# Two graph-attention layers in one kernel: layer ends that add each half of a product from its own PSUM tile, an overflow table counted inside layer 1, and prelude weight steps placed one block later

## The chip, the cores and the metric

The kernel runs on one core of a Trainium2 chip. The metric is the device time of one execution in microseconds (us), and of several executions the median is taken. Inside a profile, times are counted from the first instruction of the execution.

## The reference

There are N = 2708 nodes with 1024 features each, and an adjacency matrix `adj` of 2708 x 2708 integers, about 17 neighbours to a node. Two attention layers follow each other, and each ends with a residual and a layer normalisation. Cut to what matters:

```python
f = x @ Wf + bf;  g = x @ Wg + bg            # layer 0
e = relu(f @ g.T)
attention = softmax(where(adj > 0, e, NEG), axis=1)
x = layernorm(x + attention @ (x @ W + bW))

h = x @ W1                                   # layer 1
e = leaky_relu(h @ a1 + (h @ a2).T, 0.2)
attention = softmax(where(adj > 0, e, NEG), axis=1)
x = layernorm(x + relu(attention @ h))
```

## The kernel before

The matrix is sparse, so nothing of size N x N is multiplied. The kernel turns each row of `adj` into a list of up to 40 neighbour numbers, sorts the nodes by the length of their lists, cuts them into 22 blocks (the first of 20 nodes, held in 32 rows, then 21 of 128), and gathers the neighbours' rows from memory. A block has four groups of 32 nodes. One gather brings 128 rows of 1024 numbers: 4 neighbours for each of the 32 nodes of a group. In total there are 405 such gathers in each layer.

Five engines work, each on its own queue in the order in which the program names the instructions (the class `InOrder` pins that order). In the profile nearly all instructions bear line 71, the line of that class, so they are told apart by their tiles.

- **Prelude** (the loop over `b` under `steps = weights()`). `lists(b)` loads a block of 128 rows of `adj` (three buffers), takes its relu and row sums on ScalarE, multiplies it with a ramp of column numbers on GpSimd (line 409), and takes the 40 largest values of each row on VectorE (`nc.vector.max` and `match_replace`, lines 412 to 418). `keep_lists` writes finished lists to memory from ScalarE. Beside it the generator `weights()` folds the weights: M = Wf Wg^T, and the vectors that come from the biases and from a1 and a2. It transposes on TensorE, copies out of PSUM on ScalarE, and multiplies on TensorE. It is cut into 21 steps by `yield`; the loop takes one step after each `lists(b)`, starting with block 0. The last steps are the rows for the bias (`c_product(1)`, cut in three by `row_parts` on GpSimd), eight transposed quarters of W1 (`turned`), and `u_product`.
- **Sort.** On the finished counts, VectorE and TensorE compute each node's place (line 452 to 499), which yields `ids`, the node numbers of each block.
- **Layer 0** (loop over `units`, order 1, 0, 2, ..., 21). `load_x` gathers the block's own rows, `x_turn` transposes them, `f_product` multiplies with M, `replicate` copies the result four times, `dots` takes one scalar product for each gathered tile on VectorE, and `soft` makes the softmax weights `st`. `sums` multiplies the same gathered tiles with `st` on TensorE into `po`; ScalarE scales that into `y`; `turn` transposes `y` (ScalarE copies it into `yTs`), and a `product` with W gives `Wp[b]`. `close(b)` adds the residual (`load_residual`), normalises (`norm`), takes the scalar products with `u1b` and `u2b` (`dot`, one instruction each on VectorE), writes the row to `X1S`, and scatters row and scalar product into the table `T1`. Each block's product and `close` run one unit late: `back` is the block before. The gathers go through a ring of 20 slots (`lay.gathers()`), and a slot is free when `sums` is done with it.
- **Layer 1** gathers from `T1`, whose rows carry their score, so `scores1` needs no scalar products. `sums`, `turn` and a `product` with M (which now holds W1) follow, then `close1`: relu, residual, `norm`, and a scatter into the output. The ring has 32 slots (`ring` and `more`). The first gather of layer 1 can't start before the last scatter into `T1` has landed.
- **Overflow test.** The lists have room for `TILES[g]` entries in each group. At the end of layer 1 the table `over` is set to 1 where a list must hold nothing (88 `memset`s on GpSimd), multiplied with the lists and counted on VectorE, summed on TensorE and copied by ScalarE into `flag`. All engines then read `flag` (`values_load`) and jump over the general path, which is only taken for other graphs.

A `product` makes both halves (512 columns each, one PSUM bank each) in one tile `pm` of the pool `ps_m`, which has two buffers. A reader of the tile waits for the whole tile. At the end of a layer the whole of the last product is therefore on the way before the residual is added:

```python
        Wp[b] = product(nrows[b], yTs.pop(b)[0], Wt, 32)
        ...
            dve.tensor_add(z[:n, :D], flat(Wp.pop(b))[:n], z[:n, :D])
            steps = norm(z, n)
```

Of the kernel before, what the change touches and what calls it, by code (L numbers as in the profile page):

```python
# [8 lines left out]
F32 = mybir.dt.float32  # L9
# [3 lines left out]
ALU = mybir.AluOpType  # L13
AX = mybir.AxisListType
# [43 lines left out]
TILES = [SORTED[_g] for _g in GROUPS]  # L58
# [48 lines left out]
def listed_path(ctx, tc, x, adj, Wf, bf, Wg, bg, W, bW, W1, a1, a2, out):  # L107
# [86 lines left out]
    with tc.tile_pool(name="pre", bufs=1) as pre:  # L194
# [54 lines left out]
        with tc.tile_pool(name="adjp", bufs=3) as adjp, tc.tile_pool(name="cands", bufs=2) as cands, \  # L249
# [185 lines left out]
            for b in range(NB):  # L435
                lists(b)
                if b > 2:
                    keep_lists(b - 3)
                if b == 4:
                    fill_highs()  # L440
                next(steps, None)
            for b in range(NB - 3, NB):
                keep_lists(b)
            for _ in steps:
# [96 lines left out]
    def half_product(pm, h, n, xT, w, row=None):  # L541
# [3 lines left out]
        for k in range(KC):  # L545
            pe.matmul(pm[:n, h, :], xT[:, k, :n], w[:, k, c],
                      start=(row is None and k == 0), stop=(k == KC - 1))

    def split_product(xT, w, parts, row=None):

        pm = ps_m.tile([P, H, 512], F32, name="pm")
        for h in range(H):
            c = slice(h * 512, (h + 1) * 512)
            if row is not None:
                pe.matmul(pm[:32, h, :], ones3[row:row + 3, :32], rows3[row:row + 3, c], start=True, stop=False)
            for k in range(KC // Q):
                for p in range(Q):
                    i = p * KC // Q + k  # L560
                    pe.matmul(pm[32 * p:32 * p + 32, h, :], xT[:, i, :32], w[:, i, c],
                              start=(k == 0 and (row is None or p > 0)), stop=(k + 1 == KC // Q))
        act.copy(parts, flat(pm))
        yield
        pm = ps_m.tile([P, H, 512], F32, name="pm")
        for h in range(H):
            pe.matmul(pm[:, h, :], rep, parts[:, h * 512:(h + 1) * 512], start=True, stop=True)
        return pm
# [13 lines left out]
            out=table, out_offset=bass.IndirectOffsetOnAxis(ap=idx, axis=0), in_=src,  # L582
            in_offset=None, bounds_check=N - 1, oob_is_err=False)

    def norm(z, n):


        st = small.tile([P, H, 6], F32, name="bst")
        mv = small.tile([P, 2], F32, name="mv")
        for h in range(H):  # L590
            dve.bn_stats(st[:n, h, :], z[:n, h * 512:(h + 1) * 512])
        dve.bn_aggr(mv[:n], st[:n])
        var, r, t = (small.tile([P, 1], F32, name=s) for s in ("var", "rstd", "newton"))
        dve.tensor_scalar(var[:n], mv[:n, 1:2], EPS, None, op0=ALU.add)
        ri, ti = r.bitcast(I32), t.bitcast(I32)
        dve.tensor_scalar(ti[:n], var.bitcast(I32)[:n], 1, None, op0=ALU.logical_shift_right)
        dve.tensor_scalar(ri[:n], ti[:n], -1.0, float(0x5F3759DF), op0=ALU.mult, op1=ALU.add)
        for _ in range(3):
            dve.tensor_scalar(t[:n], var[:n], r[:n], r[:n], op0=ALU.mult, op1=ALU.mult)
            dve.tensor_scalar(t[:n], t[:n], -0.5, 1.5, op0=ALU.mult, op1=ALU.add)  # L600
            dve.tensor_scalar(r[:n], r[:n], t[:n], None, op0=ALU.mult)
        sh = small.tile([P, 1], F32, name="sh")
        dve.tensor_scalar(sh[:n], mv[:n, 0:1], r[:n], -1.0, op0=ALU.mult, op1=ALU.mult)
        yield
        act.activation(z[:n, :D], z[:n, :D], AF.Identity, bias=sh[:n], scale=r[:n])
# [141 lines left out]
    with ExitStack() as s0s:  # L747
# [10 lines left out]
        def load_x(b):  # L758
            xb[b] = xp.tile([P, D], F32, name="xb") if b > 0 else zs[:, :D]
            gather(pool, xb[b][:nrows[b]], x, ids[:nrows[b], b:b + 1])  # L760

        def dot(a, v, n, col):
            j = jp.tile([P, D], BF16, name="j")
            dve.scalar_tensor_tensor(j[:n], a, 1.0, v[:n], op0=ALU.mult, op1=ALU.mult, accum_out=col)
# [52 lines left out]
        def close(b):  # L817

            n, m, z = nrows[b], valid[b], Z.pop(b)
            dve.tensor_add(z[:n, :D], flat(Wp.pop(b))[:n], z[:n, :D])  # L820
            steps = norm(z, n)
            next(steps)
            yield
            for _ in steps:
                pass
            sp.dma_start(X1S[start[b]:start[b] + m, :], z[:m, :D])
            yield
            dot(z[:n, :D], u1b, n, f1[:n, b:b + 1])
            dot(z[:n, :D], u2b, n, z[:n, D:D + 1])
            yield  # L830
            if z is not zs:
                pool.memset(z[:, D + 1:], 0.0)
            scatter(T1[:, :], ids[:m, b:b + 1], z[:m])
# [9 lines left out]
        load_lists(0)  # L843
        q_dot(1)
        q_dot(0)
        lay.most = len(units[0].tiles)
        first_gathers(1, 5)
        x_turn(1)
        spread0, spread1 = q_spread(0), q_spread(1)
        next(spread1)  # L850
        load_x(2)
        load_lists(2)
        lay.most += len(units[1].tiles)
        first_gathers(0, 1)
        x_turn(0)

        halves, xT = [], xTs.pop(1)
        for h in range(H):
            halves.append(ps_m.tile([P, H, 512], F32, name="pm"))
            half_product(halves[h], h, P, xT, M, 0)  # L860
        pool.memset(zs[:, D:], 0.0)
        load_lists(3)
        next(spread0)
# [27 lines left out]
        for k, u in enumerate(units):  # L891
# [18 lines left out]
            next(closing, None)  # L910
            for r in reps[1:3]:
                replicate(nxt.b, r)
            lay.sums(u, po, {12: [lambda s=closing: [None for _ in s]]}, y[b])
            closing = iter(())
            if ahead is not None and not first:
                x_turn(ahead)
            if k + 3 < NB and not first:
                loaded = seq[k + 3]
                load_x(loaded)
            if back is not None:  # L920
                load_residual(back)
                if back > 0:
                    Wp[back] = product(P, yTs.pop(back)[0], Wt, 32)
                else:
                    Wp[back] = whole(split_product(yTs.pop(back)[0], Wt, frp.tile([P, D], F32, name="Fr"), 32))
# [11 lines left out]
            steps = turn(y[b], nrows[b], yT, halves=True)  # L937
            next(steps)
            yTs[b] = yT, steps
            if k + 4 < NB and not first:  # L940
                load_lists(seq[k + 4])
            if nxt is not None:
# [9 lines left out]
        load_residual(b)  # L952
        for _ in yTs[b][1]:
            pass
        Wp[b] = product(nrows[b], yTs.pop(b)[0], Wt, 32)
        for _ in closing:
            pass
        for _ in close(b):
# [3 lines left out]
    with ExitStack() as s1s:  # L962
# [38 lines left out]
        def close1(b):  # L1001
            m, xt, z = valid[b], x1[b % 2], z1[b % 2]
            sp.dma_start(xt[:m], X1S[start[b]:start[b] + m, :])
            dve.scalar_tensor_tensor(z[:m], flat(prod.pop(b))[:m], 0.0, xt[:m], op0=ALU.max, op1=ALU.add)
            for _ in norm(z, m):
                pass
            yield
            scatter(out, ids[:m, b:b + 1], z[:m])

        lay.gathers()  # L1010
        scores1(units[0])
        closing = iter(())
        waiting = []
        for k, u in enumerate(units):
            nxt = units[k + 1] if k + 1 < len(units) else None
            b = u.b
            back = b - 1 if b > 0 else None
            po = ps_s.tile([P, H, 512], F32, name="po")
            y[b] = yp.tile([P, D], F32, name="y1")
            if back is not None:  # L1020
                for _ in yTs[back][1]:
                    pass
            lay.sums(u, po, {6: [lambda s=closing: [None for _ in s]]}, y[b])
            closing = iter(())
            if back is not None:
                if back > 0:
                    prod[back] = product(P, yTs.pop(back)[0], M)
                else:
                    prod[back] = whole(split_product(yTs.pop(back)[0], M, z1[1]))
            yT = tp.tile([P, KC, P], F32, name="yT")  # L1030
            steps = turn(y.pop(b), nrows[b], yT, halves=True)
            next(steps)
            yTs[b] = yT, steps
            if waiting:
                closing = close1(waiting.pop())
                next(closing)
            if back is not None:
                waiting.append(back)
            if nxt is not None:
                scores1(nxt)  # L1040
        for _ in closing:
            pass
        b = NB - 1
        for _ in yTs[b][1]:
            pass
        prod[b] = product(nrows[b], yTs.pop(b)[0], M)
        for b in waiting + [b]:
            for _ in close1(b):
                pass


        over = ovp.tile([P, NG, QT], F32, name="over")
        pool.memset(over, 0.0)
        for g in range(1, NG):
            if TILES[g] < QT:
                pool.memset(over[:, g, TILES[g]:], 1.0)
        for q in range(Q):
            pool.memset(over[32 * q:32 * q + valid[0], 0, TILES[0]:], 1.0)
        dve.scalar_tensor_tensor(over, SL, float(N), over, op0=ALU.is_lt, op1=ALU.mult)
        dve.tensor_reduce(bad[:, 0:1], over, AX.XY, ALU.add)  # L1060
        dve.tensor_reduce(bad[:, 0:1], bad, AX.X, ALU.add)
        pt = ps_t.tile([P, 4, P], F32, name="pt")
        pe.matmul(pt[0:1, 0, 0:1], bad[:, 0:1], ones, start=True, stop=True)
        act.copy(flag, pt[0:1, 0, 0:1])
    return nc.values_load(flag[0:1, 0:1])


@with_exitstack
def general_path(
# [360 lines left out]
```

## Time and profile before

| what | value |
|---|---|
| median of 3 runs | 1803.02 us (1797.66 to 1807.29) |
| span of the profiled execution | 1799.5 us |
| prelude | about 0 to 207 us |
| sort and first block | about 207 to 282 us |
| layer 0 | about 282 to 1173 us |
| layer 1 up to its last gather | about 1178 to 1726 us |
| what follows the last gather | about 1726 to 1799.5 us |
| busy: PE, DVE, ACT, POOL | 1573.3, 1172.8, 636.4, 1187.0 us |

The stages have different limits, and so the shares over the whole span (TensorE 87%) say little; each part of the change has to be read in its own stretch. In the rows of a timeline the columns are start, duration, engine, line, operation with output and input, count, and in brackets how long the engine had been idle and what ended that. A row of several instructions gives their time in sum or from first to last. "PEld" are the weight loads of TensorE. POOL is GpSimd; `DMA_INDIRECT` on POOL is the issue of one gather or scatter. In the chain of waits a row is start, duration, and the work or transfer that the end depended on.

### The profile page before, as it was taken

The numbers are of one execution on the slowest core, as the hardware profiler recorded it, in microseconds if no ns is written. First come the engines' busy times: TensorE is split into PE (matmuls) and PEld (weight loads), VectorE is DVE, ScalarE is ACT, GpSimd is POOL, SyncE is SP. The second block draws the span as 40 slices with busy tenths as digits, with TensorE's granted clock in tenths as the row PEclk, the third lists the DMA queues.
The fourth block names the chain that finished last, engine by engine and source line by source line (L and its number), as shares of the span: only waits on it lengthen the run. The fifth ranks groups of instructions, "written<-read, shape, count | busy, mean of one in ns | idle before, by whom it ended". The sixth has DMA issues, their size and how long they took to land. (4 is left out here: it accounts for less than half of the span.)

```text
span 1799.5 us, 22910 instructions
## 1 busy us (share of the span) xinstructions
PE 1573.3 (87%) x7313; PEld 669.9 (37%) x7313; DVE 1172.8 (65%) x3537; ACT 636.4 (35%) x861; POOL 1187.0 (66%) x1191
## 2 busy tenths in 40 slices
PE   5999279899999999999999997828989889889995
PEld 3544124343444443444444443303333333333332
DVE  4879737888888888888888887422442433433442
ACT  5545354444445545445554444101111111111110
POOL 7888476567666666766666653067777777777741
PEclk9999679899999999999999998959999999999997
DMA  7747068568777777777777786189999999999960
GB/s 267 262 151 261 20 238 303 209 211 292 292 262 263 261 262 260 278 276 287 289 293 275 260 292 227 71 339 368 362 394 393 393 360 396 392 391 381 370 229 26
DMA packets 149982, 501.86 MB, mean 279 GB/s; under 512 B 32565, under 2 KB 32597, under 8 KB 147144
## 3 DMA queue, kind: packets, MB, share of 16 engines
q0 software_dynamic: 132032, 427.36, 64.2%
q1 hardware_dynamic: 10202, 55.72, 8.2%
q10 hardware_dynamic: 7618, 17.23, 2.7%
q8 instruction: 59, 0.97, 0.2%
q14 instruction: 71, 0.58, 0.1%
HBM read 509.64 MB, written 33.75 MB: 302 GB/s over the span
## 5 line engine op out<-in xcount | busy, mean ns | idle before, releaser
L71 POOL DMA_INDIRECT ring<-in_x_dram,SL x405 | 439.9, 1086 | 258.2 <-issue 97.9
L71 DVE SCALAR_TENSOR_TENSOR j<-ring,Fr 128x1024 bf16<-128x1024 f32 x402 | 495.2, 1232 | 81.8 <-DMA ring<-in_x_dram,SL 55.6
L71 ACT COPY Fr<-pm 32x1024 f32<-32x1024 f32 (+2 forms) x353 | 340.7, 965 | 21.0 <-PE pm L71 16.3
L71 PE MATMUL po<-ring,st 128*32 128x512 f32 x2660 | 340.6, 619 | 0.1
L71 POOL DMA_INDIRECT ring<-T,SL x260 | 259.4, 998 | 84.9 <-issue 57.2
L71 PE MATMUL pm<-M,xT 128*128 128x512 f32 (+1 forms) x704 | 311.5, 622 | 0.4 <-ACT xT L71 0.4
L71 PE MATMUL pm<-Wt,xT 128*128 128x512 f32 (+1 forms) x704 | 303.5, 599 | 0.0
L71 PE MATMUL pm<-M,yT 128*128 128x512 f32 (+1 forms) x704 | 298.5, 595 | 0.3 <-ACT yT L71 0.3
L71 ACT ACTIVATE scores<-scores 128x24 f32<-128x24 f32 (+5 forms) x44 | 9.8, 222 | 667.7 <-DVE scores L71 667.7
L71 PEld LDWEIGHTS pm<-M,xT 128*128 128x128 f32 (+1 forms) x704 | 127.3, 191 | 172.1 <-issue 171.4
L71 PEld LDWEIGHTS pm<-M,yT 128*128 128x128 f32 (+1 forms) x704 | 127.2, 186 | 170.2 <-issue 169.7
L71 PEld LDWEIGHTS pm<-Wt,xT 128*128 128x128 f32 (+1 forms) x704 | 125.0, 186 | 151.8 <-issue 151.6
L71 POOL DMA_INDIRECT more<-T,SL x145 | 144.7, 998 | 44.6 <-issue 32.6
L71 PEld LDWEIGHTS po<-ring,st 128*32 128x32 f32 x2660 | 104.9, 115 | 185.6 <-issue 182.4
L71 DVE TENSOR_SCALAR scores<-ring,f1q 128x2 f32<-128x2 f32 (+5 forms) x98 | 21.7, 241 | 209.9 <-DMA ring<-T,SL 208.3
L409 POOL TENSOR_TENSOR adj<-adj,iota 128x2708 f32<-128x2708 f32 (+3 forms) x23 | 130.5, 5686 | 21.5 <-ACT adj L71 21.4
L71 ACT ACTIVATE y<-po,ri 128x512 f32<-128x512 f32 (+1 forms) x88 | 55.9, 684 | 221.4 <-PE po L71 203.9
L412 DVE MAX8 cand<-adj 128x8 f32<-128x136 f32 (+2 forms) x440 | 96.6, 285 | 36.3 <-POOL adj L409 36.3
L71 PE MATMUL pt<-rs,stack 128*32 128x1 f32 x680 | 13.8, 177 | 118.0 <-DVE rs L71 68.8
L71 PE MATMUL pm<-halfT,WfT 128*128 128x512 f32 x256 | 112.5, 594 | 1.5 <-ACT WfT L71 1.5
L71 POOL DMA_INDIRECT SL<-LD,idq x85 | 86.0, 1012 | 25.8 <-issue 20.9
L71 PE MATMUL po<-more,st 128*32 128x512 f32 x580 | 91.7, 639 | 0.0
(198 smaller groups left out, 1411.9 us busy)
## 6 DMA issues: line engine op xcount, KB each, us to landing
adj<-in_adj_dram SPq DMA_DIRECT2D x21, 1354.0 KB, 6.0
X1S<-z SPq DMA_DIRECT2D x20, 512.0 KB, 6.3
ring<-in_x_dram,SL POOLq DMA_INDIRECT x405, 6.4
u1b<-X1S SPq DMA_DIRECT2D x11, 512.0 KB, 7.1
rb<-X1S SPq DMA_DIRECT2D x10, 512.0 KB, 7.2
ring<-T,SL POOLq DMA_INDIRECT x260, 7.3
rows<-in_L_gnn_Wg_dram ACTq DMA_DIRECT2D x8, 512.0 KB, 6.4
rows<-in_L_gnn_Wf_dram ACTq DMA_DIRECT2D x8, 512.0 KB, 3.4
```

Of the source, the lines that this page charges most:

```text
L71: made = self.tc.keep_in_program_order(op(*args, **kwargs))
L409: nc.gpsimd.tensor_tensor(k[:n, cut], k[:n, cut], iota[:n, cut], op=ALU.mult)
L412: nc.vector.max(cand[:n, s, :], k[:n, s * SEG:min((s + 1) * SEG, N)])
```

## The change

It has five parts, called A to E below.

- **A**, prelude: the step of `weights()` after block 0 is left out, so each step stands behind the relu of the next block in ScalarE's queue, and the last step comes after the loop.
- **B**, start of layer 0: the first seven gathers of the first unit are issued, then the own rows of block 2 (`load_x(2)`), then the other eight.
- **C**, end of layer 0: the transposed `y` of block 20 is copied out at once; the product of block 20 and the rest of `close(19)` come ahead of the sums of block 21, where before they came after them; the last product is made in two PSUM tiles, and each half is added and taken into the statistics (`bn_stats`) by itself; in `close` the scalar product with `u2b`, which the scatter into `T1` needs, comes ahead of that with `u1b`.
- **D**, the table `over`: it is marked by GpSimd in small groups of `memset`s between the gathers of layer 1, counted before the sums of block 12, and `flag` is read by the engines in unit 20.
- **E**, end of layer 1: the last product in two tiles as in C, and nothing is left to do after the last scatter.

```diff
@@ prelude
-                next(steps, None)
+                if b > 0:
+                    next(steps, None)
@@
+    def two_products(n, xT, w, row=None):
+        halves = [ps_m.tile([P, H, 512], F32, name="pm") for h in range(H)]
+        for h in range(H):
+            half_product(halves[h], h, n, xT, w, row)
+        return halves
@@
-    def norm(z, n):
+    def norm(z, n, made=None):
...
         for h in range(H):
+            if made is not None:
+                made(h)
             dve.bn_stats(st[:n, h, :], z[:n, h * 512:(h + 1) * 512])
@@ close(b)
-            dve.tensor_add(z[:n, :D], flat(Wp.pop(b))[:n], z[:n, :D])
-            steps = norm(z, n)
+            pm = Wp.pop(b)
+            def add(h):
+                c = slice(h * 512, (h + 1) * 512)
+                dve.tensor_add(z[:n, c], pm[h][:n, h, :], z[:n, c])
+            if b + 1 < NB:
+                dve.tensor_add(z[:n, :D], flat(pm)[:n], z[:n, :D])
+            steps = norm(z, n, None if b + 1 < NB else add)
...
+            dot(z[:n, :D], u2b, n, z[:n, D:D + 1])
             dot(z[:n, :D], u1b, n, f1[:n, b:b + 1])
-            dot(z[:n, :D], u2b, n, z[:n, D:D + 1])
@@ start of layer 0
-        lay.most = len(units[0].tiles)
+        lay.most = len(units[0].tiles) // 2
         first_gathers(1, 5)
...
         load_x(2)
+        lay.most = len(units[0].tiles)
+        lay.gathers()
@@ unit loop of layer 0
+            if nxt is None:
+                for _ in closing:
+                    pass
+                load_residual(back)
+                Wp[back] = product(P, yTs.pop(back)[0], Wt, 32)
             lay.sums(u, po, {12: [lambda s=closing: [None for _ in s]]}, y[b])
...
-            if back is not None:
+            if back is not None and nxt is not None:
                 load_residual(back)
...
             yTs[b] = yT, steps
+            if k + 2 == NB:
+                for _ in steps:
+                    pass
@@ after it
-        Wp[b] = product(nrows[b], yTs.pop(b)[0], Wt, 32)
+        Wp[b] = two_products(P, yTs.pop(b)[0], Wt, 32)
@@ layer 1 (close1 has an add(h) of the same kind)
+        def mark_over(b):
+            for g in groups[b]:
+                if g == 0:
+                    for q in range(Q):
+                        pool.memset(over[32 * q:32 * q + valid[0], 0, TILES[0]:], 1.0)
+                elif TILES[g] < QT:
+                    pool.memset(over[:, g, TILES[g]:], 1.0)
...
         lay.gathers()
+        pool.memset(over, 0.0)
         scores1(units[0])
...
+            if k == NB // 2 + 1:
+                count_over()
             lay.sums(u, po, {6: [lambda s=closing: [None for _ in s]]}, y[b])
...
+            for i in (2 * k, 2 * k + 1):
+                if i < NB:
+                    mark_over(i)
+            if k + 2 == NB:
+                unfit = nc.values_load(flag[0:1, 0:1])
...
-        prod[b] = product(nrows[b], yTs.pop(b)[0], M)
+        prod[b] = two_products(P, yTs.pop(b)[0], M)
...
-        over = ovp.tile([P, NG, QT], F32, name="over")
...
-    return nc.values_load(flag[0:1, 0:1])
+    return unfit
```

More of the change, by code (lines that the diff above doesn't have):

```diff
@@ L855, in listed_path @@
         x_turn(0)
[L857 to L860, printed above, removed]
+        halves = two_products(P, xTs.pop(1), M, 0)
         pool.memset(zs[:, D:], 0.0)
@@ L1003, in close1, with add @@
             sp.dma_start(xt[:m], X1S[start[b]:start[b] + m, :])
-            dve.scalar_tensor_tensor(z[:m], flat(prod.pop(b))[:m], 0.0, xt[:m], op0=ALU.max, op1=ALU.add)
-            for _ in norm(z, m):
+            pm = prod.pop(b)
+            def add(h):
+                c = slice(h * 512, (h + 1) * 512)
+                dve.scalar_tensor_tensor(z[:m, c], pm[h][:m, h, :], 0.0, xt[:m, c], op0=ALU.max, op1=ALU.add)
+            if b + 1 < NB:
+                dve.scalar_tensor_tensor(z[:m], flat(pm)[:m], 0.0, xt[:m], op0=ALU.max, op1=ALU.add)
+            for _ in norm(z, m, None if b + 1 < NB else add):
                 pass
@@ L1008, in close1, with count_over @@
             scatter(out, ids[:m, b:b + 1], z[:m])
+        over = ovp.tile([P, NG, QT], F32, name="over")
+        def mark_over(b):
[5 more added lines that the diff above has]
+                    pool.memset(over[:, g, TILES[g]:], 1.0)
+        def count_over():
+            dve.scalar_tensor_tensor(over, SL, float(N), over, op0=ALU.is_lt, op1=ALU.mult)
+            dve.tensor_reduce(bad[:, 0:1], over, AX.XY, ALU.add)
+            dve.tensor_reduce(bad[:, 0:1], bad, AX.X, ALU.add)
+            pt = ps_t.tile([P, 4, P], F32, name="pt")
+            pe.matmul(pt[0:1, 0, 0:1], bad[:, 0:1], ones, start=True, stop=True)
+            act.copy(flag, pt[0:1, 0, 0:1])
         lay.gathers()
+        pool.memset(over, 0.0)
         scores1(units[0])
@@ L1049, in listed_path @@
                 pass
-        over = ovp.tile([P, NG, QT], F32, name="over")
[L1053 to L1064, printed above, removed]
-    return nc.values_load(flag[0:1, 0:1])
+    return unfit
 @with_exitstack
```

## The prediction

> **What bounds the kernel now.** I read the 40 slices, then windows by stage, then the chain of waits, and the timeline where the chain changes engine.
>
> ```profile
> PE   5999279899999999999999997828989889889995
> POOL 7888476567666666766666653067777777777741
> ```
>
> TensorE (PE) is full in layer 0 (slices 6 to 24), nearly idle at the change of layers (slice 25), and GpSimd (POOL) stands at one constant level all through layer 1. The windows of layer 1 (window, length, busy time of PE, PEld, DVE, ACT, POOL with counts, clock, DMA share, GB/s) sharpen that:
>
> ```profile
> 1300.00:1420.00 120.00, 107.65 (x561) 43.72 (x560) 42.57 (x177) 15.94 (x30) 91.63 (x93) 0.94 1.01 393
> 1420.00:1540.00 120.00, 107.06 (x618) 44.88 (x620) 49.20 (x205) 15.79 (x32) 91.56 (x93) 0.99 0.99 382
> ```
>
> Each holds 93 POOL instructions, 120 / 93 = 1.29 us for each: 0.99 busy and the 0.30 that the timeline shows ahead of nearly each gather. So layer 1 is paced by the issue of gathers, and the DMA engines are about full too. What delays the first gather, or takes POOL's time between gathers, goes into the end. How a short memset lies between gathers is seen once, in layer 0:
>
> ```profile
> 259.37 1.02 POOL L71 DMA_INDIRECT ring<-in_x_dram,SL  x1 [0.30 <-issue]
> 260.39 0.12 POOL L71 MEMSET z<- 128x4 f32 x1
> 260.69 1.01 POOL L71 DMA_INDIRECT SL<-LD,idq  x1 [0.19 <-issue]
> ```
>
> The next issue begins 1.32 us after the last one, so this memset lay within the 0.30 and cost about 0.01. The chain at the change of layers (start, duration, what):
>
> ```profile
> 1122.64 9.72 PE po L71 x60
> 1132.36 14.76 PE pm L71 x34
> 1147.12 0.87 PE pt L71 x8
> 1147.99 14.78 PE pm L71 x34
> 1162.79 1.24 DVE ring L71
> 1164.05 1.30 DVE bst L71 x2
> ...
> 1169.99 1.25 DVE j L71 x2
> 1171.26 1.24 DVE j L71 x2
> 1173.37 3.44 DMA T<-ring,ids
> ```
>
> Sums of block 21, product of block 20, transposes, product of 21, addition, statistics, two scalar products, last scatter. The first product belongs to a block that was ready at 1111, while PE waited 11.1 us for the softmax of block 21 (the wait of the transposes' tile for DVE rs). The chain's end:
>
> ```profile
> 1778.00 1.24 DVE z L71
> 1779.26 1.30 DVE bst L71 x2
> ...
> 1785.39 0.97 POOL out_dram L71
> 1786.36 0.83 POOL over L71
> 1787.24 2.88 POOL over L71 x84
> 1790.57 1.06 DVE over L71
> ```
>
> After the last scatter (issued by 1786.36) come 7.0 us for the table, up to the flag at 1793.40, then the jump, to 1799.5. In the prelude, ScalarE's (ACT's) relus of the last two blocks:
>
> ```profile
> 181.55 2.47 ACT L71 ACTIVATE adj<-adj 128x2708 f32<-128x2708 int32 x1
> 188.33 2.46 ACT L71 ACTIVATE adj<-adj 20x2708 f32<-20x2708 int32 x1
> ```
>
> Both had their data already; they stood behind copies of the weight steps. The sort's first matmul ran at 207.09, after PE had waited 18.8 us for the counts. So lists, not weights, end the prelude, yet PE is busy 59.1 of 60 us from 60 to 120 and 57.3 from 120 to 180.
>
> **What the Trainium skill says.** "TensorE: Matmul & The Clock Gate", section on the HAM clock gate: an idle array falls to half its clock, and about 3.4 us of work release it. The trace agrees: after the 11.1 us of waiting the sums took 9.90 us for 60 matmuls (clock 0.70), where block 20's took 7.05 for 64 (clock 1.00). "DMA: Bandwidth & Descriptors", section on one DMA of the GpSimd path: the fixed cost is mostly the completion of the write, about 2 us. Here the scatter into T1, 1.00 us of issue, kept the next gather waiting 3.24 us more. "Runtime: NRT & Kernel Launch", section on instruction fetch: a jump out of the fetched window stalls until its target is fetched. Here PE's jump at 1794.0 took 4.35 us, the other engines' under 0.1.
>
> **The change part by part.**
>
> *C, order.* Block 20's transposes end at 1111.1. ACT is idle then (its last copies end at 1107.5), so two copies of some 0.6 us let the product begin at about 1111.5; its PSUM buffer is the one those copies had emptied. It takes 14.76, to about 1126.4, 4.1 us past the softmax (1122.3), since `sums` stands behind it. Then 0.3 + 7.05 for the sums at full clock (the product has kept PE busy): 1133.8. Now `y`, its transposes and copies lie bare, where before the other product covered them: in the first unit of layer 0 sums ended at 289.1 and the second half's transposed copy at 291.8, of which the product, starting with the first half, needs about 2.6. Then 14.7: 1151.1, against 1162.79: 11.7 saved. If the sums stay at 9.90 it is 8.9.
>
> Does DVE keep up? `close(19)` still adds at 1122; its scatter (1132.45, with the new order of dots 1.27 earlier) frees `z`, the residual of 20 lands by about 1140, `close(20)` runs 9.5 us (1147.16 to 1156.73 before), to about 1149.5. It is ahead of the second half at 1151.1, with little to spare.
>
> *C, halves.* After the last matmul DVE does half of 1.24 and one bn_stats of 0.65 in place of 1.24 + 1.30: 1.25 saved; the first half lies beside the second product. *C, dots.* One dot, 1.27, leaves the path of the scatter; `u1b` runs while the scatter is on its way. C together: 11.7 + 1.25 + 1.27 = 14.2 (8 to 15). As layer 1 is a steady issue from its first gather, all of it arrives.
>
> *E.* Halves again 1.25. The table's 7.0 us leave the end. POOL then reads the flag after its scatter (0.50 in the trace), jumps, and the end waits for the scatter's landing: issue begin + 4.2 as for T1, which is near the 1799.5 - 1793.4 = 6.1 us that still follow. PE's slow jump moves behind the norm. E together 8.3 (6 to 9).
>
> *D.* 88 memsets, 4.18 us, go between gathers, in one of 850 columns (0.83) and 11 groups of eight. Beyond the first they came every (4.18 - 0.83) / 87 = 0.039 us, so a group is 0.31, about the gap that hid the memset above. Net: 0.83 - 0.30, and little for the groups; I take 1.0. Lower bound 0, upper 4.2. Reading 1.0 rests on one memset in one gap. The count adds 2.25 us on DVE (1.05 + 1.04 + 0.16) ahead of block 12's sums; queued behind it are the reciprocal and `close1`, and PE waits for it with one small matmul. Who waits for PE is the gather that needs its slot: in units 2 to 4 a slot's next gather came 6 to 8 us after the sums began, so 2.3 us are hidden. The read of the flag stands on PE ahead of block 21's sums: 0.5 us, of which 0.3 was idle; on the other engines it lies in waits of over 2 us. I count 0.2.
>
> *A.* Gain: at the end, block 21's relu no longer stands behind block 20's relu (2.8 with its accumulator and list) and the `u_product` copies (3.5 and gaps): 188.33 - 181.6 = 6.7. Cost: at the start ACT waits for the second block's load before it issues the weights' loads, so PE, which began at 14.57, begins about 4.5 later (loads of 1354 KB pass in 5 us), and PE has few idle microseconds to recover it in. Also GpSimd's `row_parts` (6.7 us) now sit between the last two line-409 multiplications, which holds the gain under 5.6. I take 3.5 (from 6 gained to 2 lost). The `u_product` copies that now come last end before ACT is needed by the sort.
>
> *B.* DVE's dots begin 6 to 7 us earlier (they waited for block 2's rows, 9.3 us until 255.33). But PE's `f_product(2)` ends at 281.5, after the softmax at 280.2, and does not depend on them. Nothing gained: PE's work hides it.
>
> Sum: -14.2 - 8.3 + 1.2 - 3.5 = -24.8; 1803.0 - 24.8 = 1778.
>
> **The rivals.**
>
> 1. *The prelude gives nothing.* PE is the bound there and the 4.5 us at its start stay. For it: 59 of 60 us busy; against: PE waited 18.8 at the end. 1803 - 14.2 - 8.3 + 1.2 + 1 = 1783.
> 2. *GpSimd takes the table in full and the layer end saves less:* memsets drain the issue (4.2), PE stays cold (C at 9). For it: the issue paces layer 1; against: the memset at 260.39. 1803 - 9 - 8.3 + 4.4 - 3.5 = 1787.
> 3. *DMA paces layer 1* (share 1.01), so the memsets are free, and the prelude's lists gain 5.6: 1803 - 15 - 9 + 0.2 - 5.6 = 1774. Against it: the issue comes like a clock at 1.29 to 1.30, and the gathers land in 7.2 to 7.3 us at the median, hardly more than the 6.4 of layer 0.
> 4. *Slower:* each of twelve memset stretches costs a whole issue slot, 12 x 1.3 = 15.6, the prelude loses 4.5, the order of C gains nothing beyond halves and dots (2.5) as `close(20)` waits for its residual, E gains 6: 1803 + 15.6 + 4.5 - 2.5 - 6 = 1815. Against it: all of the above lines.
>
> **How the numbers follow.** Forecast 0.55, rival 1 0.15, rival 2 0.13, rival 3 0.14, rival 4 0.03. The predicted time is the forecast's, 1778. The range reaches from 1769 (rival 3 and 5 us for the spread of runs, which was 1797.66 to 1807.29) to 1790 (rival 2 and some of that spread). The limit of 0.5% is 1794; rivals 1 to 3 all lie below it, so faster 0.93, same 0.04, slower 0.03.
>
> **What would show each step right or wrong.** C: the product of block 20 in the gap before block 21's sums, those at about 7 us, and the last scatter into T1 near 1156 on a prelude that is 3.5 us earlier (1173.4 - 14.2 - 3.5). D: 93 issues in 120 us still, and gaps of 0.3 to 0.4 around the groups; gaps of 0.6 or more would be rival 2. A: the sort's first matmul near 203.5; near 208, rival 1. B: the first sums still right after `f_product(2)`. E: nothing but the jump after the last scatter, about 6 us. The forecast fails if the sums of block 21 stay at 10 us, or a wait for the residual appears ahead of the last addition.

## The result and the profile after

| | before | changed |
|---|---|---|
| median | 1802.55 us (6 runs, 1797.66 to 1812.86) | 1779.38 us (6 runs, 1775.26 to 1786.32) |
| ratio, 95% interval | | 0.9881 [0.9857, 0.9906] |
| span of the profiled execution | 1799.5 us | 1777.1 us |

The changed kernel is faster by 23.2 us, within 2 us of the forecast. The parts do not agree as well as the sum, as the same views show. First the page's 40 slices of the changed kernel, PE and POOL:

```profile
PE   4999479899999999999999999637989988989996
POOL 7878476467666666666666663177777777777740
```

The hole at the change of layers is still there (slices 26 to 28 of 40; before, it was deepest in slice 27, which the prediction calls 25), and layer 1 still stands at one level. Its windows (window, length, busy time with counts of PE, PEld, DVE, ACT, POOL, clock, DMA share, GB/s):

```profile
1300.00:1420.00 120.00, 111.90 (x640) 43.93 (x637) 46.98 (x193) 14.80 (x29) 92.72 (x133) 0.93 1.01 392
1420.00:1540.00 120.00, 108.63 (x571) 44.35 (x570) 44.24 (x179) 17.03 (x32) 92.26 (x108) 0.96 0.99 380
```

POOL's count is 133 and 108 where it was 93: the memsets. Its busy time has grown by 1.1 and 0.7 us, more than nothing. The timeline of POOL around two groups:

```profile
1202.19 0.99 POOL L71 DMA_INDIRECT ring<-T,SL  x1 [0.31 <-issue]
1203.19 0.80 POOL L71 MEMSET over<- 20x7 f32 x8
1204.58 1.00 POOL L71 DMA_INDIRECT ring<-T,SL  x1 [0.59 <-issue]
...
1248.96 0.99 POOL L71 DMA_INDIRECT ring<-T,SL  x1 [0.30 <-DVE rstd L71]
1249.95 0.37 POOL L71 MEMSET over<- 128x3 f32 x8
1250.47 1.00 POOL L71 DMA_INDIRECT ring<-T,SL  x1 [0.15 <-issue]
```

From gather to gather it is 1250.47 - 1248.96 = 1.51 us in place of 1.30, and 2.39 at the first group. Half of the gap before a gather remains behind a memset, so a group isn't hidden in it. At the end of layer 0, PE's timeline shows the order that C wanted:

```profile
1110.65 7.13 PE L71 MATMUL pm<-Wt,xT 128*128 128x512 f32 x16
1117.72 0.31 PE L71 MATMUL pt<-rs,stack 128*32 128x1 f32 x16
1117.87 7.05 PE L71 MATMUL po<-ring,st 128*32 128x512 f32 x60
1125.77 1.23 PE L71 MATMUL pt<-ident,y 128*128 128x128 f32 x8 [0.86 <-ACT y L71]
...
1134.63 7.13 PE L71 MATMUL pm<-Wt,xT 128*128 128x512 f32 x16
```

The product of block 20 fills the former gap, the sums of block 21 take 7.05 us (9.90 before), and only 0.86 us of waiting is left in the row. The chain of waits there (start, duration, what):

```profile
1127.34 4.29 DMA z<-in_x_dram,ids
...
1131.72 1.24 DVE z L71
...
1141.37 0.61 DVE ring L71
1142.01 0.69 DVE bst L71
1142.70 0.60 DVE ring L71
1143.33 0.70 DVE bst L71
...
1148.68 1.24 DVE j L71 x2
...
1150.70 5.88 DMA T<-ring,ids
```

It now runs through the residual of block 20 and `close(20)`. The timeline of DVE and POOL shows the wait for that residual, and the scatter of block 19 that stands ahead of its gather:

```profile
1131.72 1.23 DVE L71 TENSOR_TENSOR z<-pm,z 128x1024 f32<-128x1024 f32 x1 [8.30 <-DMA z<-in_x_dram,ids]
```

```profile
1122.35 1.87 POOL L71 DMA_INDIRECT T<-z,ids  x1 [18.03 <-DVE j L71]
1127.34 1.03 POOL L71 DMA_INDIRECT z<-in_x_dram,ids  x1 [3.13 <-DMA T<-z,ids]
```

`close(20)` frees DVE at 1141.37, when PE is nearly done (about 1141.8). The addition and statistics of the first half still stand in front of the second half, whose addition begins at 1142.70: 0.9 us after its product was ready. The last row of the chain is the surprise: 5.88 us for the scatter's transfer, where 3.44 stood before. At the end of the program:

```profile
1762.02 0.70 DVE z L71
...
1762.75 0.71 DVE bst L71
...
1768.61 0.70 POOL out_dram L71
```

Half a row is added in 0.70 us in place of 1.24, and the last scatter is the chain's last row. ScalarE's relus of the last two blocks of the prelude:

```profile
176.80 2.46 ACT L71 ACTIVATE adj<-adj 128x2708 f32<-128x2708 int32 x1 [3.96 <-DMA adj<-in_adj_dram]
189.30 2.46 ACT L71 ACTIVATE adj<-adj 20x2708 f32<-20x2708 int32 x1
```

Block 20's comes 4.75 us earlier than before and now waits for its data alone, block 21's 0.97 later, and the sort's first matmul, 207.09 before, is at 207.46. By stages, with three later executions that are told of below (us; each row is the time from the event of the row above it, and each column adds up to its span):

| up to | before | changed | `after_again` | `best` | `a_lead` |
|---|---|---|---|---|---|
| sort's first matmul, from the start | 207.09 | 207.46 | 205.65 | 203.83 | 204.03 |
| first sums of layer 0 | 74.47 | 72.67 | 72.85 | 72.55 | 72.35 |
| sums of block 20 | 806.71 | 800.06 | 807.64 | 807.70 | 808.95 |
| first gather of layer 1 | 89.34 | 77.19 | 77.68 | 75.48 | 77.24 |
| issue of the last scatter | 607.78 | 610.95 | 609.08 | 607.89 | 608.80 |
| end | 14.13 | 8.72 | 8.41 | 8.09 | 8.10 |

So four questions stood open: where 6.65 us inside layer 0 came from, which the change hardly touches; what A gives; why the scatter lands later; what D costs.

### The profile page after: what moved, and what is told of

Same layout as the page of the kernel before. It is cut to its first block, busy times and chain, and to the rows that moved or that the text cites. A ratio compares the mean times of both kernels' runs of the same rounds, so it can differ in the third digit from the quotient of the medians.

```text
span 1777.1 us, 22911 instructions
## 1 busy us (share of the span) xinstructions
PE 1573.1 (89%) x7313; PEld 667.6 (38%) x7313; DVE 1171.4 (66%) x3539; ACT 636.4 (36%) x861; POOL 1182.5 (67%) x1191
## 5 line engine op out<-in xcount | busy, mean ns | idle before, releaser
L71 POOL DMA_INDIRECT ring<-in_x_dram,SL x405 | 432.0, 1067 | 256.2 <-issue 89.0
L71 PE MATMUL pt<-rs,stack 128*32 128x1 f32 x680 | 14.1, 179 | 98.0 <-DVE rs L71 53.4
```

What stands on the lines that cost most here:

```text
L71: made = self.tc.keep_in_program_order(op(*args, **kwargs))
```

## The experiments

**Parts alone.** Three kernels were the kernel before with only A, B or C of the diff, the fourth with D and E; the fifth was the kernel before again.

> Only A: the weight step of the prelude stands behind the next block's relu, all else as before. Theory from the two traces: nothing, 1802 us within 2. The weight rows are then asked for 3 us later, TensorE makes its first product some 6 us later, and the lists' first stages lose what the earlier relus gain: the sort's first matmul stays within 1 us of 207.1. Rival, the prediction's own step: 3.5 us less, 1799, with that matmul near 203.5. Second rival: A carries part of the 8 us by which the changed kernel leads at the end of layer 0, so 1797 or less.

> Only B: seven gathers of the first tiles, the load of block 2's rows, then the other gathers. Theory: the first sums come 0 to 1.5 us earlier (281.6 before) and the time is 1801 to 1803 us. Rival: B sets another phase between gathers and sums and is what made layer 0 drift ahead by 6.7 us more before its last block; then 1794 to 1796, with the sums of block 20 starting near 1080 and not near 1088.

> Only C: the end of layer 0 (product of block 20 ahead of the sums of block 21, halves in two PSUM tiles, dot with u2b first). Theory: the last scatter of T1 is issued some 14.5 us earlier counted from the sums of block 20, some 2 us of it is given back in the wait for its landing, and the time is 1790 us (1788 to 1792), with block 20's sums where they were before (1088, within 2). Rival: C is also where the drift inside layer 0 comes from, then block 20's sums start near 1081 and the time is near 1783. Second rival: the wait gives back all but 8 us, 1795.

> Only D and E: overflow table in layer 1, halves at its end, layer 0 and prelude as before. Theory from the two traces: the memset groups between the gathers cost layer 1 3.7 us, the end gives 6.5 us, together 2.8 us less, 1800 us (1798 to 1801). Rival, the prediction's steps: groups 1.0 and end 8.3, 1795. Second rival: gathers are hidden behind TensorE in layer 1 and D is free while E is 6.5: 1796.

> The kernel before once more, for a second trace of it. If the 6.7 us by which the changed kernel gains inside layer 0 (from the sums of unit 5 to those of block 20) are a difference between executions, this trace has block 20's sums some us away from 1088.3, within 1081 to 1095, with no edit at all. If they belong to A, B or C, it repeats 1088 within 1 us. On a chip whose clock is throttled as in the four runs of single parts, the first sums come near 290 instead of 281.6, and layer 1 takes some 750 us instead of 610.

They went to a chip that grants TensorE a mean clock of 0.90 to 0.91 where the first one granted 0.95. The kernel before takes 2006.74 us there (median of all 75 runs; 1985.00 in the one run of `before_again`), and no part could be told from nothing in the time: A 0.9967 [0.9928, 1.0006], B 1.0021 [0.9984, 1.0059], C 0.9963 [0.9915, 1.0012], D with E 1.0026 [0.9988, 1.0065]. PE's timeline in layer 1 of the run with A shows why C and D couldn't count there:

```profile
1601.60 11.00 PE L71 MATMUL pm<-M,yT 128*128 128x512 f32 x25
1613.55 0.59 PE L71 MATMUL pm<-M,yT 128*128 128x512 f32 x1 [0.95 <-issue]
...
1617.08 0.59 PE L71 MATMUL pm<-M,yT 128*128 128x512 f32 x1 [1.54 <-issue]
1619.18 1.01 PE L71 MATMUL pm<-M,yT 128*128 128x512 f32 x1 [1.51 <-issue]
```

Single matmuls of the product stand 1 to 1.5 us apart with nothing that they wait for. TensorE paces layer 1 on that chip: in the 120 us from 1240 GpSimd waited 16.4 us for TensorE's sums (15.2 to 20.6 us in the other four traces of that chip, 1.8 in the kernel before on the first chip), and there were 75 POOL instructions where 93 had been. An earlier first gather is then only waiting. `before_again` met the same chip, with block 20's sums at 1131.5, so its own question stayed open there. Distances inside a trace are what these runs can tell:

- C: from the sums of block 20 to the first gather of layer 1 77.34 us, against 89.05, 89.47, 88.20 and 87.70 in the four kernels without it. From the issue of the last scatter to that gather 6.67, against 4.2 to 4.4 in the others. So both the gain and what is given back come with C.
- E: from the last scatter to the end 8.36 us, against 13.98 to 14.41.
- Layer 0 from its first sums to those of block 20: 839.1 (the kernel before), 852.0 (D with E, which leave layer 0 as it was), 845.4 (B), 849.5 (C), 863.3 (A). One and the same code differs by 13 us here. The rival that A, B or C carries the 6.65 us had no support: none of the three had a shorter stretch than the kernel before.

**The scatter's landing.** Three edits of the changed kernel. `u1_first` undoes one part of C:

```diff
-            dot(z[:n, :D], u2b, n, z[:n, D:D + 1])
             dot(z[:n, :D], u1b, n, f1[:n, b:b + 1])
+            dot(z[:n, :D], u2b, n, z[:n, D:D + 1])
```

> The changed kernel with one part of C undone: the dot with u1b again ahead of the dot with u2b. Measured from the issue of the last scatter into T1 to the first gather of layer 1, which was 4.24 us before and 6.68 after the change. Theory: what follows the scatter so closely (the dot with u1b on DVE, and the 512 KB load into u1b that this dot releases) slows its descriptors or its data; here both are out of the way ahead of it, so 4.2 us again, the scatter 1.27 us later, and the first gather some 1.2 us earlier than in the changed kernel: about 76.0 us after the start of block 20's sums instead of 77.2. Rival: the longer wait comes with C's order (the write of X1S or the chain's place), then 6.7 stays and the first gather is 1.2 us later, 78.4.

`u1_late` holds the last block's dot with `u1b` behind the scatter:

```diff
             dot(z[:n, :D], u2b, n, z[:n, D:D + 1])
-            dot(z[:n, :D], u1b, n, f1[:n, b:b + 1])
+            if b + 1 < NB:
+                dot(z[:n, :D], u1b, n, f1[:n, b:b + 1])
...
             scatter(T1[:, :], ids[:m, b:b + 1], z[:m])
+            if b + 1 == NB:
+                pool.memset(f1[:n, b:b + 1], 0.0)
+                dot(z[:n, :D], u1b, n, f1[:n, b:b + 1])
```

> The changed kernel with the last block's dot with u1b held until GpSimd has issued the last scatter into T1 (a memset of its result column stands behind the scatter on GpSimd). Theory: the scatter has neither the dot nor the load beside it, so its issue is 1.0 and not 1.34 us and the whole 4.2 to 4.6 us instead of 6.68; first gather about 75 us after the start of block 20's sums instead of 77.2. Rival: the wait belongs to the write of X1S, still 2 us ahead, then 6.7 stays.

`x1_late` moves only the load:

```diff
-            sp.dma_start(xt[:m], X1S[start[b]:start[b] + m, :])
+            (act if b == 1 else sp).dma_start(xt[:m], X1S[start[b]:start[b] + m, :])
```

> The changed kernel with the load of block 1's rows of X1S into u1b asked for by ScalarE where the block is closed, instead of by SyncE as soon as the dot with u1b is done; the dots stay as they are. Theory of the load: its 512 KB share the DMA engines with the scatter's 522 KB, so the time from scatter issue to first gather falls from 6.68 to 4.3 to 4.6. Theory of the dot: [...]6.7 stays with the issue at 1.34. If both share in it, about 5.5.

The timeline of the changed kernel first, all engines, then POOL in `u1_late` and in `x1_late`:

```profile
1149.94 1.23 DVE L71 SCALAR_TENSOR_TENSOR j<-ring,u1b 128x1024 bf16<-128x1024 f32 x1
1150.70 1.34 POOL L71 DMA_INDIRECT T<-ring,ids  x1 [8.33 <-DVE j L71]
...
1151.20 0.33 SPq L71 DMA_DIRECT2D u1b<-X1S  x1
...
1157.38 1.03 POOL L71 DMA_INDIRECT ring<-T,SL  x1 [5.34 <-DMA T<-ring,ids]
```

```profile
1232.54 1.00 POOL L71 DMA_INDIRECT T<-ring,ids  x1 [8.32 <-DVE j L71]
1233.54 0.11 POOL L71 MEMSET f<- 128x1 f32 x1
1236.85 1.03 POOL L71 DMA_INDIRECT ring<-T,SL  x1 [3.20 <-PE pt L71]
```

```profile
1236.36 1.34 POOL L71 DMA_INDIRECT T<-ring,ids  x1 [8.32 <-DVE j L71]
1240.93 1.03 POOL L71 DMA_INDIRECT ring<-T,SL  x1 [3.23 <-DMA T<-ring,ids]
```

| | scatter's issue | then waiting | issue to first gather | block 20's sums to first gather |
|---|---|---|---|---|
| before | 1.00 | 3.24 | 4.24 | 89.34 |
| changed | 1.34 | 5.34 | 6.68 | 77.19 |
| `u1_first` | 1.00 | 3.49 | 4.49 | 77.02 |
| `u1_late` | 1.00 | 3.20 | 4.31 | 75.25 |
| `x1_late` | 1.34 | 3.23 | 4.57 | 75.18 |

The load is the cause of 2.1 us: with the dot where it was and only the load gone, the wait is 3.23 again. SyncE asks for 512 KB into `u1b` as soon as the dot has read it, half a microsecond after the scatter's issue began, and the two transfers share the engines. The Trainium skill ("DMA: Bandwidth & Descriptors", section "Issuing engines are not separate DMA queues") says just this: DMAs started by different engines run on the same DMA engines and interleave. The dot itself costs the 0.34 us of longer issue, which is absent wherever it doesn't run beside the scatter. That agrees with one rule of the Trainium skill's "SBUF — State Buffer", section "Who interferes with whom": a VectorE instruction with two SBUF inputs contends with a GpSimd instruction that reads SBUF. The dot is such an instruction. But the same section infers that a `tensor_tensor` with two such inputs leaves the writing of DMA descriptors alone; here the measurement decides, and what in the issue was held is not shown. The longer the two run together, the longer the issue: 0.47 us beside the dot gave 1.34, and in the changed kernel the scatters of blocks 19 and 20, 0.98 and 0.99 us beside their dots, took 1.87 and 1.86 (1.02 before). So the new order of the dots has a second price, which the prediction left out: from the issue of block 19's scatter to the gather of block 20's residual it was 4.99 us in place of 3.67, and DVE waited for that residual. `u1_first` came 0.17 earlier where 1.2 was expected, as its scatter was issued 2.02 us later and not 1.27: the old order also holds block 19's scatter, and with it the residual of block 20 and `close(20)`, so that the last dots began 0.66 later already. The new order of the dots is thus worth 2.0 us at the scatter; in the changed kernel all of it goes to the load's collision, in `x1_late` 1.8 remain (77.02 - 75.18).

**The table.** `table_early` is the changed kernel with all 88 memsets ahead of `lay.gathers()` and no `mark_over`:

> The changed kernel with all memsets of the overflow table ahead of layer 1's gathers, so that they fall in GpSimd's wait for the landing of the last scatter (5.34 us, against 4.18 us of memsets), and none between gathers. Theory: the 3.7 us that D cost in layer 1 are gone: gathers 1.30 us apart from the first on, the first gather still 6.7 us behind the scatter. Rival: the table's place is still held by layer 0, or the memsets hold up the landing, and the first gather comes up to 4.2 us later, which gives the gain back.

```profile
1269.15 1.34 POOL L71 DMA_INDIRECT T<-ring,ids  x1 [8.33 <-DVE j L71]
1270.49 4.17 POOL L71 MEMSET over<- 128x850 f32 x88
1275.60 1.04 POOL L71 DMA_INDIRECT ring<-T,SL  x1 [0.95 <-DMA T<-ring,ids]
```

The memsets lie whole within the wait: 6.45 us from scatter to gather (6.68 without them), 77.32 from block 20's sums, and the next 20 gathers 1.30 us apart. The rival falls. These four runs were on a third chip, with clocks of 0.897 to 0.913 and 1992 to 2046 us beside 2069 for the kernel before, one run each, so nothing is read from their times.

**All together.** `best` is the changed kernel with the edit of `x1_late` and the memsets on DVE, between `f1q` and the first gathers:

```diff
+        over = ovp.tile([P, NG, QT], F32, name="over")
+        dve.memset(over, 0.0)
+        for g in range(1, NG):
+            if TILES[g] < QT:
+                dve.memset(over[:, g, TILES[g]:], 1.0)
+        for q in range(Q):
+            dve.memset(over[32 * q:32 * q + valid[0], 0, TILES[0]:], 1.0)
         lay.gathers()
-        pool.memset(over, 0.0)
...
-            for i in (2 * k, 2 * k + 1):
-                if i < NB:
-                    mark_over(i)
```

> The changed kernel once more, timed beside the kernel before on whichever chip this is. If TensorE keeps 0.95 of its clock, 0.988 of before. If it is throttled to 0.90, layer 1 is no longer paced by the issue of gathers but by TensorE; then the gathers' head start of C and the memsets of D count for little, E's 6.5 us and part of C stay, and the ratio is between 0.99 and 1.0.

> The changed kernel with two edits: block 1's rows of X1S asked for by ScalarE where the block is closed, and the overflow table's 88 memsets on DVE (VectorE) ahead of layer 1's first softmax, where DVE waited 13.5 us for gathers. Theory: the first gather 75.2 us after the start of block 20's sums instead of 77.2, no memset on GpSimd in layer 1 and the gathers 1.30 us apart throughout, so 5.7 us less than the changed kernel where the gathers pace layer 1 (1774 against 1779), and less than half of it on a throttled chip. Rival: [...]those come up to 4 us later or further apart than 1.30.

`a_lead` takes the first weight step of the changed kernel back to its old place and leaves out the second's: `if b != 1:` in place of `if b > 0:`.

> The changed kernel with the weight step after block 0 back in its place and the one after block 1 left out instead, so that TensorE starts as early as before and the later steps stay behind the next relu. Theory: DVE's list stages pace the end of the prelude (no idle over 0.5 us from 160 to 207 in both traces), so an earlier start of TensorE gives nothing: the sort's first matmul at 206.5 to 211, as in all traces. Rival: TensorE's and ScalarE's chain of weight steps paces it, then 3 to 6 us earlier, 201 to 204.

This chip granted 0.95 again. The changed kernel: 1781.94 us (4 runs), 0.9872 [0.9848, 0.9897], where 0.988 was expected. `a_lead`: 1781.43 us (one run). `best`: 1777.08 us (6 runs), 0.9853 [0.9827, 0.9879]. The medians are 4.9 us apart where 5.7 were expected; the runs overlap (1778.24 to 1783.18, and 1771.60 to 1784.82), so that `best` is faster than the changed kernel is not shown. Its trace shows the mechanism. DVE, then POOL:

```profile
1156.87 3.10 DVE L71 MEMSET over<- 128x850 f32 x88
```

```profile
1154.85 1.34 POOL L71 DMA_INDIRECT T<-ring,ids  x1 [8.33 <-DVE j L71]
1159.56 1.03 POOL L71 DMA_INDIRECT ring<-T,SL  x1 [3.37 <-DMA T<-ring,ids]
1160.90 1.00 POOL L71 DMA_INDIRECT ring<-T,SL  x1 [0.31 <-issue]
```

The first gather comes 75.48 us after block 20's sums, and DVE's memsets, which end at 1159.97 and so run beside the first gather's issue alone, delay nothing: the gathers follow 1.29 to 1.34 apart, and the rival falls. How far each kernel is ahead of the kernel before, by the number of the gather in layer 1 (us):

| gather | changed | `after_again` | `best` |
|---|---|---|---|
| 0 | 20.23 | 13.79 | 18.05 |
| 40 | 18.49 | 12.10 | 18.16 |
| 160 | 16.66 | 10.42 | 18.21 |
| 240 | 16.73 | 10.21 | 18.32 |
| 280 | 16.54 | 9.53 | 17.10 |
| 404, the last | 19.29 | 11.61 | 20.13 |

With memsets between the gathers 3.6 and 3.4 us are lost up to gather 160, without them none. From 240 to 280 stands the count: it puts block 12's sums back by 2.3 to 3.1 us in all of these traces; the gathers lose 0.2 and 0.7 of that, in `best`, which is further ahead of PE, 1.2. Of what the last row regains, 1.0 to 2.0 us fall at one gather, number 390, which waited 2.64 us in the kernel before and 0.68 to 1.69 in these three; for what isn't traced. The gathers' lead is not all that counts either: TensorE's last sums of layer 1 came 15.9, 11.4 and 17.1 us earlier than in the kernel before, so that 4.3, 2.4 and 1.0 us of the lead at the first gather had not arrived.

## Why the prediction was right

The sum was right within 2 us, its terms were less so: C, D and E together gave 6.4 us less than forecast (2.2, 2.5 and 1.7), and some 7 to 8 us of the measured gain belong to no term that was shown. A and B may hold part of them. That the sum still came out is luck to that extent.

- **C, order** (11.7): right. Counted from block 20's sums the last scatter came at 70.51 in place of 85.10, 14.6 us earlier with halves and dots, against 14.2 worked out. Sums at 7.05 and product in the gap, as said; PE's last product ends 12.9 us earlier, 1.2 more than forecast. The residual was not in time: the wait for it that the forecast named as a sign of failure is there, ahead of block 20's addition, and through `close(20)` it holds the last additions. From PE's end to the scatter 1.7 us were saved (10.61 to 8.94) where halves and dots were to save 2.5.
- **C, all of it arrives:** this step failed. "`u1b` runs while the scatter is on its way" was counted as free. Its end releases a load of 512 KB onto the scatter, and the first gather came only 12.15 earlier (11.66 in the second trace). The gain in layer 0's last stretch was 2.4 us smaller than its chain promised.
- **D** (1.0): mis-sized. The reading rested on one memset in one gap. A group of eight takes 0.37 and leaves 0.15 of the gap, so 0.21 for each of ten groups; the group on 20 rows cost 1.09 and the memset of 850 columns 0.67: 3.9 us, measured 3.4 to 3.6 over 160 gathers. That is nearer to rival 2's 4.2 than to the forecast; how much of it arrives at the end is less sure (the last sums above). The sign that I named, 93 gathers in 120 us, was too coarse: less the memsets the two windows still hold 93 and 92. The count was nearly hidden, as said.
- **E** (8.3): the halves 1.1 as said; of the table's 7.0 came 5.41 and 5.72, since the end now hangs on the last scatter's landing: by the trace's semaphore events GpSimd's wait for it was over 4.7 and 4.4 us after its issue, where 4.2 was taken from `T1`. The program ends 4.0 us after that wait in both traces; the forecast left 2.9 for it (14.1 - 7.0 - 4.2). Together 6.5 to 6.8.
- **A** (3.5): open, and the reasons were wrong. The first pair of traces says +0.4; the means of all traces (the table below) say -4.2, but four of the five traces without A are from one chip and only one with it is, and that one, `a_alone`, had 206.57, within the 1 us around 207.1 that its theory named. What holds in every trace: block 3's relu comes earlier with A than without, about 6 us on average, since one weight step fewer stands ahead of it, and from there to the sort 1.9 us are lost. I had put the gain at the prelude's end and the loss at its start, where TensorE began 1.3 us later (15.91) and not 4.5. At the end the last relu stands behind the copies around `row_parts` (12.5 us from relu to relu, 6.8 before), but little comes of it: from VectorE's first `max` of block 18 to the sort it is 33.05 to 33.27 us with A and 32.65 to 32.79 without. Where the rest of the 1.9 is lost isn't shown.
- **`a_lead`**: block 1's relu is at 22.0 as before and not at 10.5, and block 3's at 29.0 all the same. TensorE starts at 14.6 as before, and the sort comes at 204.03, at the edge of what the rival expected (201 to 204) and not where the theory did (206.5 to 211). But `best` had 203.83 and `after_again` 205.65 on the same chip with one and the same prelude, so this trace tells nothing below 2 us: an earlier start of TensorE gives no more than that.
- **B** (0): open within 2 us. From sort to first sums it is 1.6 to 2.1 shorter in four traces with B against one without; B alone on the other chip was 0.9 longer.
- **Layer 0's 6.65 us:** not the change. The same kernel took 807.64 there in its second trace, like the kernel before with 806.71; `best` and `a_lead` took 807.70 and 808.95. Single traces of one kernel differ by more than most parts of this change.

Rival 1's ground, that TensorE is the bound in the prelude, does not fall for its first part. In the kernel before, ScalarE's timeline at block 3's relu is:

```profile
32.12 0.59 ACT L71 COPY M<-pm 128x512 f32<-128x512 f32 x1 [4.29 <-PE pm L71]
...
33.55 2.48 ACT L71 ACTIVATE adj<-adj 128x2708 f32<-128x2708 int32 x1
```

The relu stands behind a copy that waited 4.29 us for TensorE's product. Without A it came at 33.6 and 33.7 in the two traces where TensorE's clock was 1.00 from 14 to 32 us, and at 37.2 to 39.1 in the three where it was 0.81 to 0.83; with A the clock was 0.77 to 0.91. So the size of A can't be read apart from the clock of that start. Towards the end the lists pace the prelude: from 160 us to the sort VectorE never waits longer than 0.63 us, in any trace. The prelude in all traces, whatever the chip (us):

| | relu of block 3 | from there to the sort | sort's first matmul |
|---|---|---|---|
| five traces without A | 33.55, 37.23, 37.60, 39.11, 33.73 | 173.5 to 173.7 | 207.1 to 212.8, mean 209.9 |
| eight traces with A | 30.58, 31.87, 31.30, 28.91, 29.37, 30.68, 30.05, 28.44 | 175.1 to 176.2 | 203.8 to 207.5, mean 205.7 |
| `a_lead` | 29.02 | 175.0 | 204.03 |

With C at 12, D at -3.5 and E at 6.6 the sum is 15, and 22 to 23 were measured. A may hold some 4 of the rest and B's stretch some 2, neither of them shown; the remainder is within what executions differ by and stays open.

## What to carry to other kernels

When an instruction is moved off the critical path, ask what its end releases and what it will now run beside: here the reader of a buffer let a load of 512 KB go, and it landed on the very transfer that the move was to bring forward. Work that is to hide between the issues of a paced queue is better put where that queue waits anyway, or on an engine that waits at that time. Compare distances within traces, and more than one trace of each kernel, before a few microseconds of a stage are put down to an edit.

## What the runs showed of the hardware

The same kernel took 1803 us where a mean clock of 0.95 was granted and 2007 where it was 0.90 to 0.91: some five hundredths less clock, 11% more time. The loss isn't spread evenly; in layer 1, the 120 us from 1240 had a clock of 0.73 to 0.80 in the five traces of the second chip, and of 0.96 in the first. There TensorE is the bound and not the issue of gathers, and a change that brings 1.2% on one chip couldn't be told from nothing, part by part, on the other. Eighty-eight memsets took 3.10 us on VectorE and 4.18 on GpSimd. The issue of a scatter took 1.00 to 1.02 us alone, 1.34 with 0.47 us of it beside a dot on VectorE with both inputs in SBUF, and 1.87 with 0.98 us beside one.
